# Weights prepared between the input statistics, left's zeros moved to another queue, and a new aggregation

## The chip, the cores and the metric

One core of a Trainium2 chip runs the whole program. A core has a matrix engine (TensorE; PE in the profile, PEld for its weight loads), three engines that work on 128 partitions of on-chip memory (VectorE or DVE, ScalarE or ACT, GpSimd or POOL), and SyncE (SP), which here only issues DMAs. SP and ACT each have a DMA queue of their own; both queues are served by the same 16 DMA engines. The metric is the device time of one execution in microseconds (us); the median of five runs of the kernel before is 4961.48 us (4955.7 to 4964.31).

## The reference

The input `x` has 512 x 512 places with 64 channels, in float32. Two layers are applied in turn, each as `x = x + conv(groupnorm(x))`:

```
xn    = layernorm(groupnorm(x)) over the 64 channels        # groupnorm: 32 groups of 2 channels, over all places
left  = (xn @ Wl + bl) * mask * sigmoid(xn @ Wlg + blg)     # 64 -> 128 channels
right = (xn @ Wr + br) * mask * sigmoid(xn @ Wrg + brg)
out   = sum over dd in -4..4 of  left[i+dd, i] * right[i+dd, :]      # a band of left, all columns of right
out   = layernorm(out) * sigmoid(xn @ Wog + bog)
x     = x + out @ Wo + bo
```

The groupnorm needs the mean and variance of each group over the whole of `x` before any of the layer can start.

## The kernel before, in words

The program has three parts: a preparation, layer one, layer two. A scheduler orders the plain instructions (`nc.…`) by what they depend on; instructions issued through the class `en` (line 364) are kept in the order in which the program writes them. Line 362 is the helper of that class, so everything that goes through it carries this line in the profile.

**The preparation** (`with tc.tile_pool(name="setup"…)`, lines 877 to 900) does the following. `fetch_layer` (186) loads the weights and the mask of both layers with some 68 small DMAs on ACT's queue. `solve_layer` (219) folds norm scales and biases into the weights on DVE and PE, for layer one into the tile `pack`, for layer two into `later_pack`. `input_stats` (315) reads all of `x` (67.1 MB) in 16 tiles `gn_x` of 4 MB, with three buffers, over SP's queue; for each tile DVE runs 32 `bn_stats`, one for each group (line 326). Then 32 `bn_aggr` (329) combine a partition's statistics, two small matmuls (333, 341) sum over the partitions, and `group_affine` makes the scale `ga` and the offset `gb`. `next(one)` (890) runs the generator of layer one up to its `yield`: it issues the first 14 loads of `z`, each 128 KB, on SP's queue. Then 18 DMAs of 1.2 MB (line 893) write zeros from the tile `nothing` into `left_of`, a buffer in HBM, on ACT's queue. `shifted` finishes the biases; `spare` takes `later_pack` to HBM (896), and four small DMAs (900) put zeros from `nothing` into `fewer` and `pack`.

After the preparation its pool is given back, and the tiles `XR` (memset at line 911), `ZH` (916) and `RO` lie where its tiles lay. So the first memset of `XR` has to wait for the last DMA that reads or writes the tiles underneath. On DVE it stands ahead of layer one.

**A layer** (`layer`, 693) runs over blocks of rows and chunks of columns in steps written out by hand. DVE applies `ga` and `gb` to a loaded `z`, then statistics, normalisation (POOL), transposition (PE), projection (PE), sigmoid (ACT) and so on. Among the first units are the "lefts" (`Unit` with `near`): their `z` is gathered along the diagonal; the first of them is one DMA of 127 partitions and two of one partition. DVE takes four ordinary units first, then this one.

**DMAs and semaphores.** The program gives its DMAs eight semaphores in turn, across both queues, in the order in which the scheduler places them. A DMA is issued only when the earlier DMA with the same semaphore has landed, and a queue issues in order, so an issue that waits holds back everything behind it on its queue.

Of the kernel before, what the change touches and what calls it, by code (L numbers as in the profile page):

```python
# [8 lines left out]
F32 = mybir.dt.float32  # L9
I32 = mybir.dt.int32  # L10
AF = mybir.ActivationFunctionType
ALU = mybir.AluOpType
AX = mybir.AxisListType
# [3 lines left out]
P = 128  # L17
# [36 lines left out]
def last(v: bass.AP, n: int) -> bass.AP:  # L54

    p, c = v.shape
    return v.unsqueeze(2).broadcast_to([p, c, n])
# [22 lines left out]
def tile_two_banded_layers(  # L80
# [6 lines left out]
    nc = tc.nc  # L87
# [3 lines left out]
    G = D // 2  # L91
# [36 lines left out]
    def one_bank():  # L128
        return ps.tile([P, 512], F32, tag="ps", name="bank")
# [33 lines left out]
    def views(pack: bass.AP) -> dict:  # L163
        r, at = {}, 0
        for nm, n in PARTS:
            r[nm] = pack[:, at : at + n]
            at += n
        return r
# [17 lines left out]
    def fetch_layer(i: int, w: dict, tmp) -> dict:  # L186
        def new(nm: str, shape: list, dt=F32):
            f[nm] = tmp.tile(shape, dt, name=f"{nm}_{i}")
            return f[nm]

        f = {}
        load = nc.scalar.dma_start
        new("raw", [P, 5 * H])
        new("ns", [P, 1])
        new("nb", [P, 1])
        for e in range(2):
            part = slice(e * D, (e + 1) * D)
            for n, nm in enumerate(("r", "rg", "l", "lg", "og")):
                load(f["raw"][part, n * H : (n + 1) * H], w[f"W{nm}"])
            load(f["ns"][part], col(w["norm_scale"]))  # L200
            load(f["nb"][part], col(w["norm_bias"]))
        new("brow", [1, 5 * H])
        for n, nm in enumerate(("r", "rg", "l", "lg", "og")):
            load(f["brow"][:, n * H : (n + 1) * H], row(w[f"b{nm}"]))
        load(new("osc", [H, 1]), col(w["out_norm_scale"]))
        load(new("obr", [H, 1]), col(w["out_norm_bias"]))
        load(new("wo", [H, D]), w["Wo"])
        load(new("bo", [1, D]), row(w["bo"]))
        load(new("mi", [1, L], I32), w["src_mask"])
        load(new("mq", [P, JQ], I32), w["src_mask"][0].rearrange("(q r) -> q r", r=JQ))  # L210
        nc.gpsimd.memset(new("ci", [P, JQ, NEAR], I32), 0)
        load(f["ci"][1 : P - 1], strided(w["src_mask"], JQ - WIN, (JQ, P - 2), (1, JQ), (1, NEAR)))
        m = w["src_mask"]
        for r in range(JQ):
            load(f["ci"][:1, r, WIN - r :], m[:, : NEAR - WIN + r])
            load(f["ci"][P - 1 :, r, : NEAR - 1 - r], m[:, L - NEAR + 1 + r :])
        return f
# [64 lines left out]
    def shifted(i: int, r: dict, tmp):  # L282
        add = r["add"].rearrange("p (t c) -> p t c", c=D)
        if i == 0:

            bias = tmp.tile([P, G], F32, name="bias")
            nc.vector.tensor_reduce(
                bias, add[:, 0, :].rearrange("p (g t) -> p g t", t=2), AX.X, ALU.add
            )
            nc.vector.scalar_tensor_tensor(bias, bias, 0.5, total, ALU.mult, ALU.add)  # L290
            spread(shift, bias)
        op = ALU.add if i else ALU.subtract
        nc.vector.tensor_tensor(add[:, 0, :], add[:, 0, :], shift, op)
        nc.vector.tensor_copy(add[:, 1, :], add[:, 0, :])


    def spread(o: bass.AP, v: bass.AP):

        nc.vector.tensor_copy(o.rearrange("p (g t) -> p g t", t=2), last(v, 2))
# [8 lines left out]
    def group_affine(mean: bass.AP, var: bass.AP, pool):  # L308

        ve = pool.tile([P, D], F32, name="g_ve")  # L310
        nc.vector.tensor_scalar(ve, var, GN_EPS, None, ALU.add)
        rsqrt(ga, ve)
        nc.vector.scalar_tensor_tensor(gb, mean, -1.0, ga, ALU.mult, ALU.mult)

    def input_stats():
        flat = x.rearrange("h w c -> (h w) c").rearrange("(p n) c -> p n c", p=P)
        per = L * L // P
        nt = min(128, per)
        n_t = per // nt
        with tc.tile_pool(name="gnx", bufs=3) as gx, tc.tile_pool(name="gns", bufs=1) as gs:  # L320
            st = gs.tile([P, G, n_t, 6], F32, name="gn_st")
            for t in range(n_t):
                xt = gx.tile([P, nt, D], F32, name="gn_x")
                nc.sync.dma_start(xt, flat[:, t * nt : (t + 1) * nt, :])
                for g in range(G):
                    nc.vector.bn_stats(st[:, g, t, :], xt[:, :, 2 * g : 2 * g + 2])
            mv = gs.tile([P, G, 2], F32, name="gn_mv")
            for g in range(G):
                nc.vector.bn_aggr(mv[:, g, :], st[:, g, :, :].rearrange("p t s -> p (t s)"))
            pm = one_bank()  # L330
            mean = gs.tile([P, G], F32, name="gn_mean")
            nc.vector.tensor_copy(mean, mv[:, :, 0])
            nc.tensor.matmul(pm[:, :G], lhsT=all_ones, rhs=mean, start=True, stop=True)
            tot = total
            nc.vector.tensor_scalar(tot, pm[:, :G], 1.0 / P, None, ALU.mult)
            dev = gs.tile([P, G], F32, name="gn_dev")
            nc.vector.tensor_tensor(dev, mean, tot, ALU.subtract)
            nc.vector.tensor_tensor(dev, dev, dev, ALU.mult)
            nc.vector.tensor_tensor(dev, dev, mv[:, :, 1], ALU.add)
            pv = one_bank()  # L340
            nc.tensor.matmul(pv[:, :G], lhsT=all_ones, rhs=dev, start=True, stop=True)
            var = gs.tile([P, G], F32, name="gn_var")
            nc.vector.tensor_scalar(var, pv[:, :G], 1.0 / P, None, ALU.mult)
            mc = gs.tile([P, D], F32, name="gn_mc")
            vc = gs.tile([P, D], F32, name="gn_vc")
            spread(mc, tot)
            spread(vc, var)
            group_affine(mc, vc, gs)
# [4 lines left out]
    w = views(pack)  # L353
# [523 lines left out]
    with tc.tile_pool(name="setup", bufs=1) as tmp:  # L877

        half = tmp.tile([P, P], F32, name="half")
        nc.vector.memset(half, 0.0)  # L880
        for e in range(2):
            nc.vector.memset(half[e * D : (e + 1) * D, e * D : (e + 1) * D], 1.0 / D)
        nothing = tmp.tile([P, S * (S + 2 * WIN) // 2], F32, name="nothing")
        nc.gpsimd.memset(nothing, 0.0)
        got = [fetch_layer(i, v, tmp) for i, v in enumerate(layers)]
        later_pack = tmp.tile([P, n_pack], F32, name="later_pack")
        for i, (f, r) in enumerate(zip(got, (w, views(later_pack)))):
            solve_layer(i, f, r, tmp, half)
        input_stats()
        next(one)  # L890
        z = left_of.rearrange("b (p n) -> (b p) n", n=S * (S + 2 * WIN) // 2)
        for n in range(0, z.shape[0], P):
            nc.scalar.dma_start(z[n : n + P], nothing[: min(P, z.shape[0] - n)])
        for i, r in enumerate((w, views(later_pack))):
            shifted(i, r, tmp)
        nc.scalar.dma_start(spare, later_pack)
        nc.vector.tensor_copy(fewer, w["add"])
        for to, m in ((fewer, S - 2 * WIN), (w["add"], S - WIN)):
            for e in range(2):
                nc.scalar.dma_start(to[e * S + m : (e + 1) * S], nothing[: S - m, : 2 * D])  # L900
# [40 lines left out]
def build(arrays):  # L941
    import concourse.bacc as _bacc

    nc = _bacc.Bacc("TRN2", target_bir_lowering=False, num_devices=1)
    aps = {}
    for name in _INS:
        a = arrays[f"in_{name}_dram"]
        aps[name] = nc.dram_tensor(
            f"in_{name}_dram", a.shape, mybir.dt.from_np(a.dtype), kind="ExternalInput"
        ).ap()  # L950
    out = nc.dram_tensor("out_0_dram", aps["x"].shape, F32, kind="ExternalOutput").ap()
    layers = [{n: aps[f"L{i}_conv_{n}"] for n in _NAMES} for i in range(2)]
    with tile.TileContext(nc) as tc:
        tile_two_banded_layers(tc, aps["x"], layers, out)
    return nc
# [10 lines left out]
```

## Time and profile before

| | us |
|---|---|
| median of 5 runs | 4961.48 |
| the profiled execution | 4958.23 |
| its span, from first to last instruction | 4956.4 |
| first DVE instruction of layer one on `z` | 280.88 |
| DVE busy in the whole span | 3843.0 |
| PE busy in the whole span | 4189.1 |

The span is counted from the first instruction; all stamps below are microseconds from there. The preparation takes the first 281 us, some 6% of the span. In the page's 40 slices of 124 us it is the first two and a part of the third: PE has almost nothing to do (digits 1 and 0), DVE is busy 6 and 7 tenths, and the DMA engines move 315 and 413 GB/s. After it PE is busy 9 tenths or more in nearly every slice until the end; the dip in slices 20 to 23 is the passage to layer two.

### The profile page before, as it was taken

What the parts mean: (1) busy time and instruction counts of PE and PEld (TensorE: products, weight loads), DVE (VectorE), ACT (ScalarE), POOL (GpSimd) and SP (SyncE); (2) the same over time, 40 slices, a digit from 0 to 9 for tenths busy, and PEclk for the clock granted to TensorE, in tenths of its full rate; (3) what the DMA queues carried; (4) which work ended last, traced back from release to release, by engine and by line L of the source; (5) the groups of instructions that cost most, each with busy time, mean ns of one, the idle gap of its engine ahead of it and who ended that gap; (6) DMA issues with size and microseconds to landing.
All of it is one profiled execution on the core that took longest, in us unless ns stands there. A gap on an engine that the chain in (4) does not pass through costs nothing.

```text
span 4956.4 us, 173324 instructions
## 1 busy us (share of the span) xinstructions
PE 4189.1 (85%) x67090; PEld 3549.2 (72%) x67090; DVE 3843.0 (78%) x9661; ACT 3643.8 (74%) x8156; POOL 3819.7 (77%) x4739
## 2 busy tenths in 40 slices
PE   1026899999999999999984689999999999999998
PEld 0025788888888888888763577777777777777775
DVE  6775788888888888888766578888888888888876
ACT  0013788888888888888873378888888888888888
POOL 0037888888888888888534788889889898888853
PEclk9988999999999999999997899999999999999999
DMA  7924677777777777777653467777777777777765
GB/s 315 413 65 130 180 208 202 204 208 205 205 203 204 202 205 205 207 207 207 186 147 91 130 183 205 202 205 207 209 205 207 203 207 210 205 203 206 210 183 152
DMA packets 905343, 982.32 MB, mean 198 GB/s; under 512 B 114210, under 2 KB 641608, under 8 KB 900168
## 3 DMA queue, kind: packets, MB, share of 16 engines
q1 hardware_dynamic: 897248, 948.49, 65.7%
q10 hardware_dynamic: 7272, 22.73, 1.1%
q8 instruction: 531, 8.70, 0.8%
q14 instruction: 292, 2.39, 0.2%
HBM read 658.42 MB, written 312.46 MB: 196 GB/s over the span
## 4 chain that ended last, share of the span: by engine, by line
PE 53%; ACT 16%; DVE 12%; DMA 7%; POOL 5%; issue 3%; SPq 2%; ACTq 0%; another core or an unknown queue 0%; DVEq 0%; POOLq 0%
PE banks L362 29%; PE bank L362 21%; ACT on L362 11%; DVE RO L362 4%; POOL rsqrt L362 2%; PE acc L362 2%; SPq L362 2%; DMA left_of<-nothing 2%; DVE sti L362 2%; DVE ZH L362 2%; ACT RO L362 2%; DVE XR L362 2%; POOL z L362 2%; ACT sg L362 1%; ACT gate L362 1%
## 5 line engine op out<-in xcount | busy, mean ns | idle before, releaser
L362 ACT ACTIVATE on<-RO,nm,rs 128x128 f32<-128x128 f32 x4608 | 1872.0, 496 | 129.1 <-POOL nm L362 111.4
L362 PE MATMUL banks<-pack,zT 64*128 64x256 f32 x9360 | 1323.0, 405 | 148.4 <-DVE RO L362 67.7
L362 PEld LDWEIGHTS banks<-pack,zT 64*128 64x128 f32 x9360 | 886.8, 194 | 515.9 <-DVE RO L362 220.1
L362 PE MATMUL banks<-RO,A 64*64 64x128 f32 x18432 | 1154.3, 277 | 12.7 <-ACT zT L362 12.7
L362 DVE TENSOR_TENSOR RO<-banks,sg 128x512 f32<-128x512 f32 x1152 | 790.6, 687 | 423.3 <-ACT sg L362 405.9
L362 PEld LDWEIGHTS banks<-RO,A 64*64 64x64 f32 x18432 | 1082.2, 183 | 38.5 <-ACT zT L362 15.2
L362 ACT ACTIVATE sg<-banks 128x512 f32<-128x512 f32 (+1 forms) x1188 | 694.9, 587 | 369.9 <-PE banks L362 285.0
L362 DVE BATCH_NORM_STATS2 sto<-RO 128x6 f32<-128x256 f32 x2304 | 843.3, 414 | 1.2
L362 DVE SCALAR_TENSOR_TENSOR ZH<-bank,pack,gate 128x448 f32<-128x448 f32 (+1 forms) x1152 | 738.5, 683 | 70.7 <-ACT gate L362 46.6
L362 DVE COPY RO<-banks 128x512 f32<-128x512 f32 x576 | 396.5, 691 | 486.8 <-ACT RO L362 486.3
L362 POOL TENSOR_TENSOR z<-z,gb 128x512 f32<-128x512 f32 x536 | 685.2, 1278 | 42.0
L362 PE MATMUL bank<-pack,ZH 128*64 128x64 f32 x18432 | 686.3, 229 | 5.6 <-ACT gate L362 4.9
L362 POOL TENSOR_TENSOR z<-z,ga 128x512 f32<-128x512 f32 x536 | 686.3, 1280 | 0.1
L362 POOL TENSOR_TENSOR z<-z,rs 128x512 f32<-128x512 f32 x586 | 617.2, 1053 | 46.0
L362 PEld LDWEIGHTS bank<-pack,ZH 128*64 128x64 f32 x18432 | 605.5, 142 | 47.8 <-ACT gate L362 9.0
L362 ACT ACTIVATE gate<-bank 128x448 f32<-128x448 f32 (+1 forms) x1152 | 565.6, 543 | 83.3 <-PE bank L362 71.7
L362 POOL TENSOR_TENSOR z<-z,sti 128x512 f32<-128x512 f32 x586 | 626.2, 1069 | 0.0
L362 PEld LDWEIGHTS bank<-ident,on 64*128 64x128 f32 x9216 | 410.7, 140 | 255.7 <-ACT gate L362 143.4
L362 PE MATMUL bank<-ident,on 64*128 64x64 f32 x9216 | 450.2, 228 | 134.7 <-ACT gate L362 105.9
L362 PE MATMUL bank<-zg,pack 64*128 64x448 f32 (+1 forms) x2304 | 559.7, 559 | 2.7 <-DMA zg<-later 2.2
L362 POOL TENSOR_TENSOR XR<-XR,pack 120x512 f32<-120x512 f32 (+1 forms) x352 | 418.0, 1189 | 161.2 <-DMA XR<-mid_x 63.0
L362 ACT COPY RO<-banks 128x512 f32<-128x512 f32 x576 | 333.2, 583 | 234.6 <-PE banks L362 234.5
(140 smaller groups left out, 3690.5 us busy)
## 6 DMA issues: line engine op xcount, KB each, us to landing
later<-zT SPq DMA_DIRECT2D x576, 256.0 KB
A<-left_of SPq DMA_DIRECT2D x576, 256.0 KB
zg<-later SPq DMA_DIRECT2D x576, 256.0 KB
z<-in_x_dram SPq DMA_DIRECT2D x576, 128.0 KB
z<-mid_x SPq DMA_DIRECT2D x576, 128.0 KB
gn_x<-in_x_dram SPq DMA_DIRECT2D x16, 4096.0 KB
XR<-in_x_dram SPq DMA_DIRECT2D x448, 112.0 KB
mid_x<-XR SPq DMA_DIRECT2D x448, 112.0 KB
```

The costliest lines, as they stand in the source:

```text
L362: return lambda *a, **k: tc.keep_in_program_order(f(*a, **k))
```

## The change

1. `solve_layer` is no longer called ahead of `input_stats`. `input_stats` takes a function `meanwhile` and calls it after each tile of `x`; after tile 7 it solves layer one, after tile 11 layer two. The loads of `x` and the `bn_stats` go through `en`, so they keep the order of the program.
2. The 32 `bn_aggr` and a copy become seven DVE operations on all 32 groups at once: three sums over 32 x 32 values and two elementwise operations on them, and two small ones. Each `bn_stats` leaves two triples (count, mean, sum of squared deviations), so a group has 32 means and 32 sums. One `tensor_tensor` in the sum over partitions becomes a `scalar_tensor_tensor`.
3. The 18 DMAs of zeros go from ACT's queue to SP's, through `en`: in the program's order they stand behind all loads of `x` and the 14 early loads of `z`.

```diff
-    def input_stats():
+    def input_stats(meanwhile):
...
-                nc.sync.dma_start(xt, flat[:, t * nt : (t + 1) * nt, :])
+                en.sync.dma_start(xt, flat[:, t * nt : (t + 1) * nt, :])
                 for g in range(G):
-                    nc.vector.bn_stats(st[:, g, t, :], xt[:, :, 2 * g : 2 * g + 2])
-            mv = gs.tile([P, G, 2], F32, name="gn_mv")
-            for g in range(G):
-                nc.vector.bn_aggr(mv[:, g, :], st[:, g, :, :].rearrange("p t s -> p (t s)"))
+                    en.vector.bn_stats(st[:, g, t, :], xt[:, :, 2 * g : 2 * g + 2])
+                meanwhile(t)
+            parts = st.rearrange("p g t (s k) -> p g (t s) k", k=3)
+            nm = 2 * n_t
...
+            nc.vector.tensor_reduce(mean, parts[:, :, :, 1], AX.X, ALU.add)
+            nc.vector.tensor_scalar(mean, mean, 1.0 / nm, None, ALU.mult)
+            nc.vector.tensor_tensor(off, parts[:, :, :, 1], last(mean, nm), ALU.subtract)
+            nc.vector.tensor_reduce(own, parts[:, :, :, 2], AX.X, ALU.add)
+            nc.vector.tensor_tensor(off, off, off, ALU.mult)
+            nc.vector.tensor_reduce(between, off, AX.X, ALU.add)
+            nc.vector.scalar_tensor_tensor(own, own, 1.0 / nt, between, ALU.mult, ALU.add)
             pm = one_bank()
-            mean = gs.tile([P, G], F32, name="gn_mean")
-            nc.vector.tensor_copy(mean, mv[:, :, 0])
...
-            nc.vector.tensor_tensor(dev, dev, mv[:, :, 1], ALU.add)
+            nc.vector.scalar_tensor_tensor(dev, own, 1.0 / nm, dev, ALU.mult, ALU.add)
...
-        for i, (f, r) in enumerate(zip(got, (w, views(later_pack)))):
-            solve_layer(i, f, r, tmp, half)
-        input_stats()
+
+        def meanwhile(t: int):
+
+            if t in (7, 11):
+                i = int(t == 11)
+                solve_layer(i, got[i], (w, views(later_pack))[i], tmp, half)
+
+        input_stats(meanwhile)
         next(one)
...
-            nc.scalar.dma_start(z[n : n + P], nothing[: min(P, z.shape[0] - n)])
+            en.sync.dma_start(z[n : n + P], nothing[: min(P, z.shape[0] - n)])
```

More of the change, by code (lines that the diff above doesn't have):

```diff
@@ L323, in input_stats @@
                 xt = gx.tile([P, nt, D], F32, name="gn_x")
-                nc.sync.dma_start(xt, flat[:, t * nt : (t + 1) * nt, :])
+                en.sync.dma_start(xt, flat[:, t * nt : (t + 1) * nt, :])
                 for g in range(G):
-                    nc.vector.bn_stats(st[:, g, t, :], xt[:, :, 2 * g : 2 * g + 2])
-            mv = gs.tile([P, G, 2], F32, name="gn_mv")
-            for g in range(G):
-                nc.vector.bn_aggr(mv[:, g, :], st[:, g, :, :].rearrange("p t s -> p (t s)"))
+                    en.vector.bn_stats(st[:, g, t, :], xt[:, :, 2 * g : 2 * g + 2])
+                meanwhile(t)
+            parts = st.rearrange("p g t (s k) -> p g (t s) k", k=3)
+            nm = 2 * n_t
+            mean = gs.tile([P, G], F32, name="gn_mean")
+            own = gs.tile([P, G], F32, name="gn_own")
+            between = gs.tile([P, G], F32, name="gn_between")
+            off = gs.tile([P, G, nm], F32, name="gn_off")
+            nc.vector.tensor_reduce(mean, parts[:, :, :, 1], AX.X, ALU.add)
[5 more added lines that the diff above has]
+            nc.vector.scalar_tensor_tensor(own, own, 1.0 / nt, between, ALU.mult, ALU.add)
             pm = one_bank()
-            mean = gs.tile([P, G], F32, name="gn_mean")
-            nc.vector.tensor_copy(mean, mv[:, :, 0])
             nc.tensor.matmul(pm[:, :G], lhsT=all_ones, rhs=mean, start=True, stop=True)
```

## The prediction

> **What bounds the kernel now.** From layer one's first step on, the built program of the change has on every engine the same order as before (I laid the two built orders side by side); so only the time at which the preparation lets layer one start can move. I read that stretch alone: first the chain of waits from 180 us on (start, us, what).
>
> ```profile
> 213.27 10.55 DVE gn_st L326 x32
> 223.84 22.35 DMA gn_x<-in_x_dram
> 246.21 10.54 DVE gn_st L326 x32
> 256.75 14.35 DVE gn_mv L329 x32
> 271.36 0.65 PE bank L333 x2
> 273.04 0.65 PE bank L341 x2
> 274.04 3.37 DMA spare<-later_pack
> 277.43 0.47 SPq L362
> 277.93 0.48 SPq L362
> 278.46 3.41 SPq L362
> 281.91 10.31 DMA z<-in_x_dram
> 292.35 0.70 DVE z L362
> ```
>
> The last tile of `x` arrives 22 us after its issue, 32 `bn_aggr` take 14.35 us, then SP, held until `spare` has landed (277.43), issues the first left's `z`, and DVE gets it at 292.35. That is the path. The list of SP's waits up to 420 us shows what held SP before:
>
> ```profile
> SPq L324 <- DMA left_of<-nothing: 120.2, 9, 22.3
> ...
> SPq L362 <- DMA spare<-later_pack: 27.5, 1, 27.5
> ```
>
> The table of stretches (last number GB/s) shows the DMA engines full while zeros and `x` share them, and empty in the aggregation:
>
> ```profile
> 190.00:200.00 10.00, 0.00 (x0) 0.00 (x0) 7.99 (x25) 0.00 (x0) 0.00 (x0) 1.00 0.99 426
> ...
> 260.00:270.00 10.00, 0.00 (x0) 0.00 (x0) 10.00 (x23) 0.00 (x0) 0.00 (x0) 1.00 0.00 0
> ```
>
> DVE's timeline (start, us, instruction, idle before it) has the rates and waits that I sum with:
>
> ```profile
> 33.18 0.26 DVE L252 TENSOR_SCALAR pack<-wo,osc 128x64 f32<-128x64 f32 x1 [8.78 <-DMA wo<-in_L_conv_Wo_dram]
> ...
> 54.43 0.55 DVE L228 TENSOR_SCALAR aug<-raw,ns 128x640 f32<-128x640 f32 x1 [8.08 <-DMA ns<-n_L_conv_norm_scale_dram]
> ...
> 213.27 31.41 DVE L326 BATCH_NORM_STATS2 gn_st<-gn_x 128x6 f32<-128x256 f32 x96 [1.88 <-DMA gn_x<-in_x_dram]
> ...
> 278.55 1.04 DVE L911 MEMSET XR<- 128x520 f32 x2 [1.08 <-DMA pack<-nothing]
> ...
> 292.35 0.69 DVE L362 TENSOR_TENSOR z<-z,ga 128x512 f32<-128x512 f32 x1 [4.52 <-DMA z<-in_x_dram]
> ```
>
> Where `x` is there, a tile costs 31.41 / 3 = 10.5 us of DVE; where zeros flow beside it, tiles come every 12.4 us.
>
> **The change, part by part.**
>
> *Statistics.* The zeros leave this stretch, so DVE sets its pace: 4.19 MB at 426 GB/s is 9.8 us of DMA against 10.5 of DVE, and with three buffers a load has 21 us for its 13 (the first: issued 0.72, landed 14.0). The weights are not where the edit writes them: they are outside `en`, and the built order puts layer one's behind tiles 0 and 1, layer two's between tiles 1 and 5. Their loads on ACT's queue and the first three `gn_x` are unmoved, so DVE still stands until 33.18 and tile 0 starts at 34.3. Then 16 x 10.54 = 168.6. In between: 1.8 (ten small operations after tile 0); 8.8 from tile 1's end (57.0) until the last mask piece of layer two is there, which the new order wants ahead of tile 2. ACT issues it at 61.3; in the timeline the sixth DMA of zeros, which has the next turn of its semaphore, went out at 65.74, so it had landed by then: 65.8. Then 3.0, 1.2 and 1.8 for the rest of layer two's weights (durations of the same lines before). End: 34.3 + 168.6 + 16.6 = **219.5, against 256.75: 37.2 earlier**. Bounds: mask there when asked for, 5 earlier; pieces that wait for a whole load of `x`, as `wo` did (issued 20.5, landed 33.2), 8 later.
>
> *Aggregation.* Gone: 14.35 and a copy. Added: five operations over 1024 elements. No row has that size; `z` at 512 elements took 0.68 and `bn_stats` at 256 took 0.415, some 1.05 ns an element, so 1.2 each; with two small ones and the two matmuls' round trips some 8.0 from the last statistics to the issue of `spare`, against 17.3 (256.75 to 274.04). Bounds 6.5 (reductions overlap) and 13 (strided reads at half speed). `spare` goes out at 227.5: **46.5 earlier**.
>
> *Zeros.* This takes it back. In the built order SP's queue is: 16 `gn_x`, 14 `z`, 18 zeros, then the first left's three DMAs. The zeros' semaphores decide when: the first two follow the `z` loads (about 205), but the third takes the semaphore of `fewer<-nothing`, the fifth, seventh and eighth those of the other three small DMAs of ACT, which go out after `spare`. In the trace of before the last of these lands at 278.55 (the release of the `XR` memset), 4.5 after `spare`'s issue; the first one's packets are over at 276.8, so it lands about 3.2 after. So zeros 3 to 18 start at 227.5 + 3.2 = 230.7, plus 1.3 to the first byte; the DMAs idle from about 212 till then. 16 x 1.18 MB = 18.9 MB. At 130 to 135 us, when the zeros' queue had the engines almost alone, they moved 426 GB/s, of which I count 422 for zeros: 44.7 us. End: **276.9, landed 277.6**. Bounds: the fastest such 5 us had 444, the slowest 10 us of the full stretch 408: 42.5 to 46.3.
>
> The Trainium skill's page "DMA: Bandwidth & Descriptors", section "Where 436 GB/s comes from", says that between HBM and on-chip memory HBM's 358 GB/s binds. The stretches here show 408 to 444 over 170 us of this traffic, and I go by them; by the page these zeros would take 52.7 us, and the sum below would end 8 us later.
>
> *Who waits for the zeros.* Two things. The first memset of `XR` waits in the built order for the last zero on all eight semaphores (before: for the four small DMAs), because `nothing` lies underneath; all DVE work of layer one is behind it, and POOL's `ZH` waits alike: 277.6 against 278.55. And the left's `z` stands behind the zeros on SP's queue. Its issue (277.93 before) comes at about 260, when zero 11 has landed, but its bytes go after the zeros'. Before, the 127-partition DMA took 13.9 us (277.93 to 291.86, when the next user of its semaphore went out) for 254 KB, while `z` of 128 KB needs a few; I read one engine working through 127 rows, some 12.4 us after its first byte's turn. So 276.9 + 12.4 + 0.5 = 289.8 against 292.35. Bounds: it lands with the zeros, and DVE's four units (9.2 us after the memset) set 287; or 13.9 after the zeros land, 291.5.
>
> The same page, section "Why a DMA increments its semaphore by 16 and not by 1", says that 127 partitions put everything on one engine. The 14 us agree; spread over 16 engines it would land with the zeros, the lower bound just given.
>
> *Sum.* 289.8 - 292.35 = **-2.5 us**, because 46.5 won before the zeros pay for 44.7 of zeros that were hidden under the statistics, and 2.3 of it is left at their end (SP was free at 277.93, first bytes 279.2; now 276.9). Everything after that shifts along. 4958.23 - 2.5 = 4955.7 for an execution like the profiled one (which has 1.83 outside its span); the median lies 3.25 above that execution, so the median goes from 4961.48 to **4959**. 0.2%, 9.9 us, is about what can be told from no change.
>
> **The rivals.**
> - *Slower: the mask pieces.* The order asks for layer two's last mask piece before tile 2, at a time when `gn_x` 4 and 5 are now both issued (61 us). If the pieces take turns with two loads, they land by 72 to 83 instead of 65.8, and since everything from tile 2 on hangs on it, the median becomes 4965 to 4976. It decides from 78 on (2.5 + 9.9 used up). For: `wo` and `ns` each waited for a whole load. Against: those were 64 or 128 rows, these are one row each, and one `gn_x` was in flight at 61.12 before, too. 12%, with a typical 4973.
> - *Faster: the zeros run early.* If the third zero did not wait for `fewer`, zeros would run from 205 to 254, under the aggregation, and layer one would start 24 us earlier: 4937. For: the edit places them there, and DMAs idle then. Against: SP's 27.5 us for `spare` shows that such a semaphore wait is real. 8%.
> - *A shorter chain:* the left lands with the zeros, -5.4: 4956; or the reductions run at half speed, +5: 4964. Both stay within 0.2%, and belong to the forecast.
>
> **How the numbers follow.** The forecast with its bounds (statistics -1 to +6, aggregation -1.5 to +5, zeros' rate -2 to +2, left -3 to +2, and a few us between medians) has 80% within 9.9 us, the slower rival 12%, the faster 8%. The range leaves out the faster rival and the upper half of the slower one: 4951 to 4971.
>
> **What would show it.** `bn_stats` back to back from about 66 us and ending near 219; five operations of 1.1 to 1.3 us; DMA engines empty from about 212 to 231 and full at over 400 GB/s until 277; SP waiting for `fewer` some 20 us; the `XR` memset released by `left_of<-nothing` near 278 after a wait of over 40 us; the left's `z` near 290. I am wrong if zeros flow before 228, if the statistics end after 230, or if layer one's steps change among themselves.

## The result, and the profile after

The changed kernel takes 4956.33 us (median of 25 runs, 4948.35 to 4963.86) against 4961.26 us of the kernel before (median of 45 runs beside them): a ratio of 0.9991, 95% interval 0.9986 to 0.9996, or 4.9 us less. The forecast was 4959, within 0.2% of before. So a rewrite that ends the input statistics 38 us earlier shortens the whole by a tenth of a per cent, and the work that follows asks where the 38 us went.

The chain of waits of the changed kernel from 180 us on (start, us, what) answers the first fence of the prediction. `bn_aggr`'s row is gone, and two rows of zeros stand where `x`'s last load stood.

```profile
179.82 38.81 DVE gn_st L373 x119
...
218.66 1.50 DVE gn_mean L336
...
227.49 2.83 DMA fewer<-nothing
...
239.90 19.94 DMA left_of<-nothing
259.86 17.52 SPq L373
...
277.43 11.59 DMA z<-in_x_dram
...
289.15 0.70 DVE z L373
```

The last statistics now end at 218.6 instead of 256.75, and the aggregation's first operation follows at once; but the chain then runs through `fewer`, the zeros and SP's queue, and comes out at 289.15 where it came out at 292.35. What held SP and VectorE is in the lists of waits (us in total, times, longest):

```profile
SPq L373 <- DMA fewer<-nothing: 20.4, 1, 20.4
...
DVE XR L927 <- DMA left_of<-nothing: 47.0, 1, 47.0
```

SP stood 20.4 us before the third zero, and VectorE 47.0 us before the first memset of `XR`. Of the first left's three DMAs the one of 127 rows went out at 256.99, in line behind the zeros. SP was then held 17.52 us in the issue of the first one-row piece, and the DMA of the chain's row at 277.43 is the second one-row piece, which lands last, behind the 127 rows. Where the 38 us were won and paid is plainest in the stretches (busy time of PE, PEld, DVE, ACT and POOL, the clock, the DMA share, GB/s). First one long stretch of the statistics, before:

```profile
110.00:204.00 94.00, 0.00 (x0) 0.00 (x0) 65.39 (x200) 0.00 (x0) 0.00 (x0) 1.00 1.01 430
```

The same stretch after, and the stretches behind the statistics:

```profile
110.00:204.00 94.00, 0.00 (x0) 0.00 (x0) 94.00 (x290) 0.00 (x0) 0.00 (x0) 1.00 0.96 381
...
220.00:230.00 10.00, 1.27 (x4) 1.00 (x4) 9.39 (x31) 0.00 (x0) 0.00 (x0) 1.00 0.18 72
...
240.00:250.00 10.00, 0.00 (x0) 0.00 (x0) 0.00 (x0) 0.00 (x0) 0.00 (x0) 1.00 1.02 425
...
260.00:270.00 10.00, 0.00 (x0) 0.00 (x0) 0.00 (x0) 0.00 (x0) 0.00 (x0) 1.00 1.01 424
```

Before, the DMA engines were full with zeros and `x` together and VectorE worked 65 of 94 us. After, VectorE works all 94. From 240 to 270 us no engine computes at all: the DMA engines write zeros, and everything else waits.

From the first left's `z` on, I compared the start of every VectorE instruction in the two profiled executions. The shift is -3.2 us from 293 to 314 us, -5.2 from 420 to 503 us, and up to 3200 us the medians of shorter stretches lie between -4.9 and -6.0. So the difference is there after the first 420 us. In the last third the two executions wander by some 6 us against each other (-5.5 to +0.6).

### The profile page after: what moved, and what is told of

It is laid out like the page before. It is cut to its first block, busy times and chain, and to the rows that moved or that the text cites. A ratio compares the mean times of both kernels' runs of the same rounds, so it can differ in the third digit from the quotient of the medians.

```text
span 4952.3 us, 173298 instructions
## 1 busy us (share of the span) xinstructions
PE 4191.8 (85%) x67090; PEld 3548.2 (72%) x67090; DVE 3835.0 (77%) x9635; ACT 3643.1 (74%) x8156; POOL 3820.7 (77%) x4739
## 4 chain that ended last, share of the span: by engine, by line
PE 53%; ACT 17%; DVE 15%; POOL 5%; DMA 4%; issue 3%; SPq 2%; ACTq 0%; DVEq 0%; POOLq 0%
PE banks L373 29%; PE bank L373 22%; ACT on L373 11%; DVE RO L373 4%; DVE gn_st L373 3%; POOL rsqrt L373 2%; PE acc L373 2%; SPq L373 2%; DVE sti L373 2%; DVE ZH L373 2%; ACT RO L373 2%; ACT sg L373 2%; DVE XR L373 2%; ACT gate L373 1%; ACT zT L373 1%
## 5 line engine op out<-in xcount | busy, mean ns | idle before, releaser
L373 PEld LDWEIGHTS banks<-pack,zT 64*128 64x128 f32 x9360 | 888.7, 194 | 517.1 <-DVE RO L373 218.6
```

The costliest lines, as they stand in the source:

```text
L373: return lambda *a, **k: tc.keep_in_program_order(f(*a, **k))
```

## The experiments: each part alone

All twelve kernels in one table. "memset" is the start of `XR`'s first memset, "left" that of the first left's `z`, both in us of the profiled execution. VectorE has 9.2 us of work between the two (four units of `z`), so left starts at whichever is later: the memset plus 9.2, or the landing of its own `z`.

| kernel | ratio to before, interval | memset | left |
|---|---|---|---|
| before | 1 | 278.55 | 292.35 |
| changed | 0.9991 [0.9986, 0.9996] | 277.78 | 289.15 |
| before + zeros on SP | 1.0027 [1.0018, 1.0037] | 295.88 | 307.32 |
| before + aggregation | 0.9975 [0.9965, 0.9985] | 271.84 | 281.05 |
| before + weights amid | 1.0002 [0.9993, 1.0011] | 279.31 | 293.03 |
| changed, zeros back on ACT | 0.9975 [0.9966, 0.9984] | 270.73 | 279.93 |
| changed, six zeros early | 0.9969 [0.9957, 0.9981] | 266.08 | 277.52 |
| changed, turns freed | 0.9962 [0.9948, 0.9975] | 264.68 | 275.95 |
| changed, storage kept | 1.0001 [0.9992, 1.0010] | 231.55 | 294.73 |
| changed, turns and storage | 0.9972 [0.9962, 0.9983] | 237.23 | 280.15 |
| changed, turns and order | 0.9984 [0.9975, 0.9992] | 275.55 | 284.75 |
| changed, all three | 0.9914 [0.9901, 0.9928] | 236.84 | 246.12 |

Three theories stood at the start: the aggregation alone yields the gain and the moved zeros take part of it back; the moved zeros yield it; or the placing of the weights does.

**The zeros alone.** Only the queue of the zeros is changed in the kernel before:

```diff
-            nc.scalar.dma_start(z[n : n + P], nothing[: min(P, z.shape[0] - n)])
+            en.sync.dma_start(z[n : n + P], nothing[: min(P, z.shape[0] - n)])
```

> The kernel before with one part of the change: the eighteen zeros of left are queued on SP behind the early part of x; statistics, weights and bn_aggr stay as they were. Theory (the zeros cost the same 44.7 us wherever they stand, once the small DMAs hold them back): the statistics lose the zeros' share of the transfers and end near 219 to 221 instead of 256.75; bn_aggr and its chain keep their 17.3 us, so spare goes out near 237; zeros 3 to 18 wait for the turn of a small ACT DMA behind it and end near 286; the first left's z starts near 299 instead of 292.35. So about 6.5 us slower than before (ratio 1.0013). Rival 1 (the move of the zeros is what gained the 4.9 us): 3 to 6 us faster. Rival 2 (the zeros run in idle transfer time, 205 to 254 us, whatever the semaphores): z near 266, about 26 us faster.

It is slower by 0.27% (4976.25 us against 4960.83 beside it, 15.4 us; left 15.0 later). The statistics end at 221.4, as forecast. The sign was right and the size less than half. The chain of waits of this kernel shows why:

```profile
238.77 3.30 DMA spare<-later_pack
...
242.09 0.47 SPq L362
...
278.19 17.31 SPq L362
...
295.54 11.66 DMA z<-in_x_dram
```

In this build the last piece of the early `z`, which stands ahead of the zeros on SP, has the semaphore turn after `spare`. SP waited 32.2 us for it, so all eighteen zeros went out behind `spare`, from 242.66 on, not sixteen from 240. Two zeros at 2.8 us and the later start make up the 8 us by which left (307.32) missed the 299 expected. That the move of the zeros gains by itself is refuted.

**The aggregation alone.** The seven operations go into the kernel before, all else stays:

```diff
-            for g in range(G):
-                nc.vector.bn_aggr(mv[:, g, :], ...)
+            nc.vector.tensor_reduce(mean, parts[:, :, :, 1], AX.X, ALU.add)
...
+            nc.vector.scalar_tensor_tensor(own, own, 1.0 / nt, between, ALU.mult, ALU.add)
```

> The kernel before with one part of the change: the seven operations on all groups in place of the 32 bn_aggr; zeros on ACT, weights ahead of the statistics. Theory (in the kernel before the path goes from the last bn_stats over the aggregation to the small DMAs and on to left's z): the stretch from the last bn_stats to the issue of spare goes from 17.3 to 8.3 us, left's z from 292.35 to about 283, and the whole to about 9 us less (ratio 0.9982). Rival (the aggregation is hidden, left's z is a matter of transfers): within 1 us of before.

It is faster by 0.25% (4948.84 us, 12.0 less), more than the 9 expected. VectorE's timeline (start, us, instruction, idle before it):

```profile
258.26 1.50 DVE L333 TENSOR_REDUCE gn_mean<-gn_st 128x32 f32<-128x1024 f32 x1
...
271.84 1.04 DVE L919 MEMSET XR<- 128x520 f32 x2 [1.47 <-DMA pack<-nothing]
...
281.05 0.68 DVE L370 TENSOR_TENSOR z<-z,ga 128x512 f32<-128x512 f32 x1
```

From the last statistics to the issue of `spare` it takes 266.57 - 258.22 = 8.35 us instead of 17.29, 8.9 less; the statistics end 1.5 later and `pack` lands 0.8 later behind `spare`, so the memset comes 6.7 earlier. The rest is a second effect that the expectation had not seen. Left's `z` row has no idle time before it, where the row of before had 4.52. In this build the semaphore turns fall otherwise, although no DMA was edited: the first left's DMAs no longer stand behind one that takes `spare`'s turn. The first two went out at 252.27 and 252.98, under the statistics, and not behind `spare` at 277.43. 6.7 + 4.5 = 11.2 of the 11.3 at left.

**The weights amid the statistics alone.** In the kernel before, the loads and `bn_stats` are held in order and the two `solve_layer` calls are made after tiles 8 and 12:

```diff
-        for i, (f, r) in enumerate(zip(got, (w, views(later_pack)))):
-            solve_layer(i, f, r, tmp, half)
-        input_stats()
+        def meanwhile(t: int):
+            if t in (7, 11):
+                i = int(t == 11)
+                solve_layer(i, got[i], (w, views(later_pack))[i], tmp, half)
+        input_stats(meanwhile)
```

> The kernel before with one part of the change: the weights' work placed between the tiles of the statistics (after the 8th and the 12th), the order of the loads and statistics held; zeros on ACT, bn_aggr. Theory (with the zeros among the loads of x the statistics are held by transfers, not by VectorE's row): the end of the statistics stays within 4 us of 256.75, the time within 4 us of before (0.9992 to 1.0008). Rival (VectorE's 21 us of work on the weights stands in the statistics' path): 8 to 20 us less.

No difference: 1.0002, left 0.7 later. The list of SP's waits and VectorE's row in this run say what sets the statistics there:

```profile
SPq L365 <- DMA left_of<-nothing: 142.8, 9, 29.6
...
247.00 10.54 DVE L365 BATCH_NORM_STATS2 gn_st<-gn_x 128x6 f32<-128x256 f32 x32 [1.89 <-DMA gn_x<-in_x_dram]
```

With the zeros among the loads VectorE waits for `x` whatever the order of its own work. The edit also moves less than it says, as the prediction saw for the changed kernel: in this run the weights' operations stand behind tiles 0 to 4 (45 to 103 us), without the edit among the statistics of the first tiles (33 to 70 us).

**The changed kernel with the zeros back on ACT.** The mirror image, one line:

```diff
-            en.sync.dma_start(z[n : n + P], nothing[: min(P, z.shape[0] - n)])
+            nc.scalar.dma_start(z[n : n + P], nothing[: min(P, z.shape[0] - n)])
```

> The changed kernel with its zeros back on ACT, where they run among the loads of x: weights amid the statistics and the seven operations stay. Theory: as the aggregation alone, about 9 us less than before, so about 4 us less than the changed kernel (4952 us): the move of the zeros to SP took back part of what the aggregation gave. Rival (the move of the zeros carries the gain): no better than before, 5 us above the changed kernel.

4948.98 us, 11.9 less than before and 7 less than the changed kernel: the same as the aggregation alone (left 279.93 and 281.05). So the aggregation carries the gain, about 12 us (at left 6.7 by itself and 4.5 by the turns that shifted with it), the weights' place carries none while the zeros flow among the loads, and the zeros' move gives 7 of the 12 back.

The parts do not simply add: alone they sum to 15.0 - 11.3 + 0.7 = +4.4 at left, and the change measured -3.2. The way from the run of the zeros alone (307.32) to the changed kernel (289.15) can be followed step by step instead. The statistics end 2.8 earlier (218.6 against 221.4); in both runs VectorE is busy 94 of 94 us there, and up to this point the two kernels differ only in part 1 of the change, so where VectorE sets the pace that part does count. The stretch to `spare` is 8.9 shorter, the first zero behind the small DMAs follows `spare`'s issue 0.5 sooner, and two zeros fewer stand behind it (5.6). That is 17.8 of the 18.2.

## The experiments: the three waits

Between 218 and 289 us three things couple the zeros to what follows, and the prediction named them: the turns of the semaphores, the storage under `XR`, and SP's order. The runs open them one by one and together. SP's order was opened only together with the turns, since a DMA that GpSimd issues has both another queue and other turns.

**Six zeros early.** The same queue, but the zeros are written behind the last tile, inside the loop:

```diff
         def meanwhile(t: int):
...
+            if t == 15:
+                next(one)
+                zeros(0, 18)
```

> The changed kernel with its zeros queued inside the loop over the tiles, right behind the last tile's statistics, still on SP and behind the early part of x. In the built order the first zero that takes the turn of a small DMA is the seventh (spare's) instead of the third (fewer's). Theory (what is let through before the small DMAs is what counts, 2.8 us for each zero): six zeros pass from about 211, twelve follow spare from about 231.5 and take 33.5 us; the XR memset moves from 277.8 to about 266, the first left's z from 289.15 to about 277, 11 to 12 us earlier. Rival (the turns hold nothing in themselves; the transfers' sum alone sets the end, as in the freed turn): as with all turns freed, 276, which this run can't tell from it; so it is judged on where the zeros stop: after six, until about 230, or not at all.

They stop after six, as in the built order: zeros 1 to 6 go out from 208.04 to 218.25, the seventh at 229.99 behind `spare`. SP's waits and VectorE's timeline:

```profile
SPq L373 <- DMA spare<-later_pack: 11.4, 1, 11.4
...
266.08 1.04 DVE L932 MEMSET XR<- 128x520 f32 x2 [35.84 <-DMA left_of<-nothing]
...
277.52 0.69 DVE L373 TENSOR_TENSOR z<-z,ga 128x512 f32<-128x512 f32 x1 [2.15 <-DMA z<-in_x_dram]
```

The memset is 11.7 and left 11.6 earlier than in the changed kernel, four zeros at 2.8 us as expected. The time is 4945.65 us (6 runs), 15.1 below before.

**Turns freed.** The five small DMAs are issued by GpSimd, whose DMAs take turns of another set of semaphores:

```diff
-        nc.scalar.dma_start(spare, later_pack)
+        nc.gpsimd.dma_start(spare, later_pack)
...
-                nc.scalar.dma_start(to[e * S + m : (e + 1) * S], nothing[: S - m, : 2 * D])
+                nc.gpsimd.dma_start(to[e * S + m : (e + 1) * S], nothing[: S - m, : 2 * D])
```

> The changed kernel with the five small DMAs (spare, twice fewer, twice pack) issued by GpSimd, whose DMAs have turns of their own, so that no zero takes its turn behind one of them; zeros still on SP, still out of storage that XR takes over. Theory (the third zero's wait for fewer holds sixteen zeros back for 20.4 us): zeros follow one another from 209 at 413 to 433 GB/s and end near 254; the XR memsets start there instead of at 277.78 and the first left's z near 266 instead of 289.15. About 23 us less than the changed kernel (4933 us). Rival (the zeros are no more on the path than the aggregation; or they lose in the statistics' last tile what they gain): 0 to 8 us less.

No zero waits for a small DMA any more, and the stretch that moved 72 GB/s in the changed kernel is full:

```profile
220.00:230.00 10.00, 1.27 (x4) 1.01 (x4) 9.39 (x31) 0.00 (x0) 2.80 (x5) 1.00 1.02 422
```

Left comes at 275.95 and the time is 4939.04 us (5 runs), 22.2 below before and 17.3 below the changed kernel. At left that is 13.2 earlier than in the changed kernel, not the 23 expected. The expectation had let all eighteen zeros run in the 44.7 us that belong to sixteen: 18 x 1.18 MB at 420 GB/s are 50.5 us, and `spare`'s 0.7 MB run beside them for another 1.7. From 211 that ends at 263, and the memset starts at 264.68.

**Storage kept.** The zeros' source lies in storage that is never given back. It fits only at a quarter of its width, so each row is read four times:

```diff
-        nothing = tmp.tile([P, S * (S + 2 * WIN) // 2], F32, name="nothing")
+        nothing = const.tile([P, S * (S + 2 * WIN) // 8], F32, name="nothing")
...
-            en.sync.dma_start(z[n : n + P], nothing[: min(P, z.shape[0] - n)])
+            k = min(P, z.shape[0] - n)
+            en.sync.dma_start(
+                z[n : n + k].rearrange("p (e n) -> p e n", e=4), mid(nothing[:k], 4)
+            )
```

> The changed kernel with one wait taken away: the source of the zeros, a quarter as wide and read four times over, lies in storage that is not given back, so that XR's memset need not wait for the zeros; the turns and SP's order stay. Theory (two waits end together: the memset at 277.8 with 11 us of work behind it, and left's z, which stands behind the zeros on SP and lands at 288.7): the memset moves to about 232, left's z stays near 289 and the time within 1.5 us of the changed kernel. Rival (the memset's wait of 47.0 us is the whole of it): left's z near 244, 40 us and more less.

```profile
231.55 1.04 DVE L930 MEMSET XR<- 128x520 f32 x2 [0.17 <-DVE gb L313]
...
294.73 0.69 DVE L373 TENSOR_TENSOR z<-z,ga 128x512 f32<-128x512 f32 x1 [53.83 <-DMA z<-in_x_dram]
...
240.00:250.00 10.00, 0.00 (x0) 0.00 (x0) 0.87 (x2) 0.00 (x0) 0.00 (x0) 1.00 1.03 385
```

The memset moves 46 us, its wait of 47.0 is gone, and nothing is gained: the wait has moved to left's `z` and is 53.8 us there. Left is even 5.6 later. Most of it is that rows of 2304 bytes move slower: 385 to 387 GB/s in the stretches from 240 to 270 us (the last line shows the first of them) against 417 to 425 in the changed kernel, which makes 4.2 us over sixteen zeros. The time, 4963.45 us, is 2.2 above before, so the expected "within 1.5 us of the changed kernel" was missed by this price of the edit itself.

**Turns and storage.** Both edits together:

> Both: small DMAs on GpSimd and the zeros' source kept. Theory: the zeros end near 254, left's z is queued behind them on SP with its 12 us on one engine and lands near 266, so the time is that of the freed turn alone within 1.5 us (about 23 us less than the changed kernel). Rival (the storage holds in its own right): 11 us less than with the freed turn alone.

```profile
237.23 1.04 DVE L930 MEMSET XR<- 128x520 f32 x2 [5.28 <-DMA spare<-later_pack]
...
280.15 0.69 DVE L373 TENSOR_TENSOR z<-z,ga 128x512 f32<-128x512 f32 x1 [33.57 <-DMA z<-in_x_dram]
```

Left comes 4.2 later than with the turns alone, which is again the narrower rows (21.2 MB at 386 instead of 420 GB/s: 4.5 us). The time of 4947.04 us is 8 above that with the turns alone, not within 1.5; with 7 and 5 runs the intervals of the two overlap. So the storage adds nothing while left's `z` stands behind the zeros on SP.

**Turns and order.** GpSimd issues the zeros, after the fifteenth tile; the small DMAs are back on ACT; the source has its full width and the storage that `XR` takes over. VectorE clears that source after the fifteenth tile (2.0 us), so that no zero can start earlier:

```diff
-        nc.gpsimd.memset(nothing, 0.0)
...
+            if t == 14:
+                en.vector.memset(nothing, 0.0)
...
-            en.sync.dma_start(z[n : n + P], nothing[: min(P, z.shape[0] - n)])
+            nc.gpsimd.dma_start(z[n : n + P], nothing[: min(P, z.shape[0] - n)])
```

> As with the three waits off, but with the zeros' source full width and out of the storage that XR takes over, as in the changed kernel: the turns and SP's order are freed, the storage is not. Theory (each of the two remaining waits holds alone): the zeros go out from about 210 and the last lands near 263 to 270, with left's z and spare beside them; the XR memset waits for it and the first left's z follows some 9 to 11 us behind (four units of VectorE's work): 272 to 281 against 289.15 in the changed kernel and 246.12 with the three waits off. Time 8 to 17 us less than the changed kernel. Rival (the storage never bound once SP's queue is free, and the gain of the three came from the queue): left's z near 246, 36 us less.

```profile
275.55 1.04 DVE L928 MEMSET XR<- 128x520 f32 x2 [42.24 <-DMA left_of<-nothing]
...
284.75 0.68 DVE L373 TENSOR_TENSOR z<-z,ga 128x512 f32<-128x512 f32 x1
```

Now left's `z` has no wait at all, and left still comes at 284.75, because the memset waits 42.2 us for the zeros. They land later than expected (the last at 275.23, expected 263 to 270). Beside them run `z` and `spare`; whether that is all of the delay was not separated. The time is 7.2 us below before and 2.7 below the changed kernel, where 8 to 17 were expected: the mechanism held, its price not.

**All three.** The same with the source of a quarter's width in storage of its own:

> The changed kernel with all three couplings gone: zeros out of kept storage, issued by GpSimd with turns of their own after the 15th of the sixteen tiles (VectorE clears their source there), the small DMAs on ACT as they were, left's z on SP with no zero ahead of it. Theory: the XR memsets follow the aggregation near 231, left's z waits for the turns of fewer and pack (231) and its 12 us on one engine, and starts near 244 to 255 (later, if the zeros beside it slow its landing) instead of 289.15: 34 to 45 us less than the changed kernel (4911 to 4922 us). Rival (what comes behind, the first writes into left, has to wait for the zeros in any case and gives the gain back): less than 25 us.

```profile
236.84 1.04 DVE L931 MEMSET XR<- 128x520 f32 x2 [4.94 <-DMA spare<-later_pack]
...
246.12 0.68 DVE L373 TENSOR_TENSOR z<-z,ga 128x512 f32<-128x512 f32 x1
```

Left comes at 246.12, 43 us earlier than in the changed kernel; the whole takes 4919.6 us, 36.7 less than it and 41.7 less than before (0.86%). The zeros still flow until 280 us, now beside the first steps of layer one; the first writes into `left_of`, which have to wait for them, go out at 291.61. At left, against the changed kernel's 289.15, the turns alone give 13.2, the turns with the order 4.4, the turns with the storage 9.0, and all three 43.0. With the turns open, storage and order are two locks on one door: each holds alone, and opening only one adds nothing to the 13.2. The time (4 runs) is within what was expected (34 to 45 less). This version beats both kernels of the case.

## Why the prediction held

The forecast ended within the range and on the likeliest case. By its own steps:

- *Statistics:* forecast end 219.5, measured 218.62. The ends fit for the reason given (VectorE sets the pace once the zeros are gone: 94 of 94 us busy). Two small misses cancel: the last mask piece was awaited until 67.17 instead of 65.8, and the tiles and weights behind it took 2.2 less than summed. The slower rival, which decided from 78 on, did not come to be:

```profile
67.17 0.18 DVE L275 CAST later_pack<-ci 128x36 f32<-128x36 int32 x1 [7.88 <-DMA ci<-in_L_conv_src_mask_dram]
```

- *Aggregation:* 8.0 us forecast, 8.35 measured. The estimate of 1.2 for an operation over 1024 elements fits the two that read densely; the three that read `st` with a step of three elements took 1.5 (`gn_mean` in the chain above is one). A dense one:

```profile
223.33 1.22 DVE L340 TENSOR_TENSOR gn_off<-gn_off 128x1024 f32<-128x1024 f32 x1
```

- *Zeros:* the third was forecast for 230.7 and went out at 230.34, behind `fewer`, after a wait of 20.4 us ("some 20"). They moved at 417 to 425 GB/s (422 taken). The end of 276.9 is a rounding off: its own terms, 230.7 + 1.3 + 44.7, give 276.7.
- *Who waits:* the memset at 277.78 (277.6 forecast), left at 289.15 (289.8). The issue of left's 127 rows came at 256.99 ("about 260"), and they had landed by 288.67, when the next DMA with their semaphore went out: 10.9 us after the memset was released.
- *Sum:* -2.5 forecast at left, -3.2 measured. The forecast of -2.5 for the whole also lies within the measured interval, 2.0 to 6.9 us less.
- *What was not in it:* after left the changed kernel gains another 2.0 us between 314 and 420 us, which the step "everything after that shifts along" had at nothing. The runs do not isolate its cause. In the same stretch the aggregation alone loses 2.4 of its 11.3, so a shift of the start is passed on only to some 2 us.

The prediction was also right for the reason it gave: what was won before the zeros is paid for the zeros, through the three couplings it named. Two things in it were weak without showing in the time. The rival "zeros run early" let the zeros flow from 205 to 254 and layer one start 24 us earlier than before, at 4937 us. With the turns freed the first zero goes out at 208.33 and the memset is held until 264.68, so left comes only 16.4 earlier than before. That the time of 4939.04 is near the rival's is in part luck: the other 6 us arise behind left or in the noise of 5 runs (interval 12 to 26 us less than before), and the runs do not say which. And nothing in the prediction said that the zeros' move costs more than it wins next to the aggregation: the forecast added all steps against the kernel before and did not ask what the change would be without that one edit. One line less in the diff makes it 7 us faster.

The Trainium skill's page "DMA: Bandwidth & Descriptors", section "Where 436 GB/s comes from", has the HBM side, 358 GB/s, bind such transfers; it gets that figure by halving a stack's rate between two cores. The program here runs on one, and this trace disagrees again, with 417 to 425 GB/s over the 30 us in which nothing but zeros flows from on-chip memory to HBM; the measurement decides. The same page's section "Why a DMA increments its semaphore by 16 and not by 1", by which 127 partitions go to one engine, fits the run of the aggregation alone, where left's rows flow by themselves from 254 to 264 us: the DMA share (next to last number) is 0.06, one engine of sixteen.

```profile
254.00:264.00 10.00, 0.64 (x2) 0.50 (x2) 9.90 (x19) 0.00 (x0) 0.00 (x0) 1.00 0.06 24
```

## What to carry to other kernels

Moving a transfer out from under a stage only helps if it finds other cover: ask what waits for its end, and follow all of semaphore turns, reused storage and queue order, because they hold one behind the other. Here freeing the turns alone won 13.2 us at left, keeping the storage alone won nothing, and only all three together won 43. When a change bundles several edits, price each of them alone; here one won 12 us, one nothing where it was tried alone, and one gave 7 back. And where a framework hands out a few semaphores in rotation, a DMA can wait for an unrelated one, and an edit elsewhere, here of VectorE's operations alone, can move that wait.

## What the runs showed of the hardware that was not expected

- SP was held in the issue of a one-row piece of left's `z` (1 KB, right behind the DMA of 127 rows) for 17.52 us (10.84 to 10.93 with narrow rows of zeros), until the zeros ahead of it on its queue were nearly through; its other issues in this stretch took 0.3 to 2.1 us. With no zeros ahead the same piece held SP for 3.11 us (aggregation alone) and 3.41 (before). An issue is thus not always cheap: here it blocked the engine that made it. What exactly it waited for no run shows.
- Zeros written from rows of 2304 bytes, each read four times, moved at 385 to 387 GB/s, those from rows of 9216 bytes at 417 to 425. Row length and repeated reading were changed together, so which of the two it is stays open.
- A VectorE operation over 128x1024 f32 that reads every third element took 1.49 to 1.52 us, one that reads densely 1.21 to 1.22.
- Issued by GpSimd beside the zeros, the 690 KB of `spare` landed 10.5 us after their issue; issued by ACT in the run of the zeros alone, with the engines idle, they landed after 3.30. Issued by ACT beside the zeros they took 9.3 (turns and order) and 8.5 (all three), so most of the delay goes with the shared engines and not with the issuer.
- In the run with all three waits off the profiled execution had a granted TensorE clock of 0.50 from 210 to 270 us where the changed kernel had 1.00; left came 43 us earlier all the same; TensorE is busy for only 6 of these 60 us. The runs of the zeros alone and of the six zeros early show 0.50 from 200 to 290 us, too.
